# A graph layer with sorted segment sums: new round borders in the first part, a carried sum in one operation, and an earlier, thinner filling of the second table

## The chip, the cores and the metric

The kernel runs on one core of one Trainium2 chip. The metric is the device time of that core in microseconds; lower is better. The time before is 4865.99 us, the median of three runs (4857.05 to 4868.12).

Engine names are those of the profile: PE is TensorE (PEld its weight loads), DVE is VectorE, ACT is ScalarE, POOL is GpSimd and SP is SyncE, which here does nothing but start transfers. SBUF is the on-chip memory, PSUM the one that PE accumulates in.

## The reference

There are 12,500 nodes with 128 features and 412,500 edges with 64 features. The edge list is sorted by `dst`, not by `src`, and the sum runs over `src`.

```python
h, q, k, v = (node_features @ W + b for W, b in ((Wn, bn), (Wq, bq), (Wk, bk), (Wv, bv)))
eh = edge_features @ We + be
src, tgt = edge_index                      # stack([src, dst])
attn_in = concatenate([q[src], k[tgt], eh], axis=-1)
hmid = leaky_relu(attn_in @ A1 + b1, 0.2)
scores = leaky_relu(hmid @ A2 + b2, 0.2)
w = softmax(scores.mean(axis=-1), axis=0)  # over all edges
out = segment_sum(w[:, None] * v[tgt], src, num_segments=num_nodes)
y = h + out
y = gamma * (y - mean(y)) / sqrt(var(y) + 1e-5) + beta
result = layernorm(x + y)
```

## The kernel before

**Two stages that run at once.** Nodes are split into 98 blocks of 128 by their source number. Edges come in 403 groups of 1,024, which is eight tiles of 128 edges.

The *record stage* (`make`) goes through the 403 groups. For each edge it works out a record of 260 numbers: 128 of the edge's hidden sum without the query part, 128 of its value row, and the source's place within its block. PE multiplies one-hot matrices by table rows (`rows`, L931 and L936) into the PSUM tile `pkv`; ACT copies that into an SBUF tile `rec` of four edge tiles (`evacuate`, L946 and L947; six such buffers); POOL then writes each tile of 128 records to DRAM with one indirect transfer (L958), to the block of its source. The places come from running counts on PE and DVE (L851 to L913); `pcs`, in PSUM, is the running count for each block. A group thus costs POOL eight of these scatters.

The *sum stage* (`sums_of`) reads the records back, now sorted by block, and adds them up. Its work comes in *units*: up to three blocks, and of each block t tiles of 128 records. For a unit, SP loads the tile `rt` (L1150) and spreads the source numbers over the partitions (L1204). PE and DVE add the query rows (L1216, L1230, L1239), DVE and ACT apply the leaky ReLU (L1249, L1253), PE multiplies by A2 and sums the heads. Then comes a short chain: a maximum on DVE (`mx`, L1305), spread by PE (L1311), reduced on DVE (`m`, L1319, and `ref`, L1320), the exponential on ACT (`w`, L1329). ACT weighs one-hot matrices with `w` (L1352) and PE sums the value rows into `psm` (L1381). Pieces of at most four tiles go through these steps. A unit starts every eight steps of a hand-made plan (`lags`), whether it has 12 tiles or 15.

**Parts and rounds.** The 403 groups are cut into three *parts* (`PARTS`, L36), each with a table in DRAM (part three uses the first table again). A part is summed in *rounds*: when the records up to a stop are made, a round may sum those tiles of each block that are certain to be full by then. The stops are group numbers. The table below is what the code works out; "units" is blocks per unit times tiles per block.

| round | stop | units before | begins at group, before | stop after | units after | begins at group, after |
|---|---|---|---|---|---|---|
| 1 | 74 | 33 of 3x5 | 74 | 74 | 33 of 3x5 | 74 |
| 2 | 127 | 33 of 3x4 | 127 | 140 | 33 of 3x5 | 140 |
| 3 | 165 | 49 of 2x6 | 167.1 | 165 | 33 of 3x5 | 187.4 |
| 4 | 225 | 33 of 3x4 | 227.1 | 225 | 33 of 3x4 | 234.9 |
| 5 | 278 | 33 of 3x4 | 278 | 278 | 33 of 3x4 | 278 |
| 6 | 307 | 33 of 3x5 | 318.1 | 307 | 33 of 3x5 | 317.3 |
| 7 | 367 | 33 of 3x4 | 367 | 367 | 33 of 3x4 | 367 |
| 8 | 403 | 33 of 3x5 | after the last group | 403 | 33 of 3x5 | after the last group |

"Begins at" is `begun` (L1773 to L1777): the stop, or later if the round before is by an estimate not through. `PACE` (12 tiles a group) and the constant 2.7 are that estimate. The steps of a round are spread evenly over the groups between its beginning and the next one's, so a round's tiles divided by these groups is the density of sum work beside the record work. What is left at the last group runs alone, then round 8, then a closing stage with the two norms.

**The order.** Everything is issued in the order of the code (`manual_schedule`): the loop at L1796 goes through six points a group of the record stage, and puts the due fills, table steps and sum steps at each. Every engine works strictly in that order.

**Carried sums.** A round adds to what the rounds before it left in DRAM (`old`, L1362). The old sum must be scaled by the ratio of two reference maxima, `by`. `total` (L1384) does that with one DVE operation for each block (L1397): old times `by` plus the PSUM sum, 128x128 each. In round 1 there is no old sum and the PSUM tile is copied (L1391).

**Fills.** The top rows of each block in the two tables are zeroed beforehand, by 49 transfers each (`fill_piece`, L567 to L574) on SP's queue. The first table's come from SBUF; the second's come from a zeroed DRAM tensor, and were placed evenly from group 74 to group 163.

**Checks of the counts.** At a stop, DVE copies the running count `pcs` out of PSUM (`counted`, L993 to L996), and compares the copy with limits loaded four groups earlier (`gated`, `certain`, `ended`, L998 to L1014).

Of the kernel before, what the change touches and what calls it, by code (L numbers as in the profile page):

```python
# [10 lines left out]
FP = mybir.dt.float32  # L11
# [5 lines left out]
ALU = mybir.AluOpType  # L17
# [4 lines left out]
P = 128  # L22
# [10 lines left out]
ROWS = 3  # L33
XA = 3
SPAN = 42
PARTS = (74, 127, 165), (225, 278, 307), (367, 403)  # L36
NP = len(PARTS)
NR = sum(map(len, PARTS))
PACE = 12
TABS = 2  # L40
WIDTH = 15
BLK = 3
# [7 lines left out]
class Plan:  # L50
# [4 lines left out]
    def __init__(self, n, e, nb, groups):  # L55
        self.n, self.e, self.nb, self.groups = n, e, nb, groups
        at = lambda c: groups * c // 403
        ends = [at(part[-1]) for part in PARTS]
        self.parts = list(zip([0] + ends[:-1], ends))

        def means(g0, g1):
            return [
                (min(e, g1 * GT * P) - g0 * GT * P) * max(0, -(-(n - b) // nb)) / n
                for b in range(nb)
            ]
# [22 lines left out]
        for p, (g0, g1) in enumerate(self.parts):  # L88
            t0 = 0
            for g in map(at, PARTS[p][:-1]):  # L90
                t = int(min(m - 4.4 * m**0.5 for m in means(g0, g)) // P) - t0
# [380 lines left out]
def sorted_path(  # L472
# [8 lines left out]
    nc = tc.nc  # L481
# [3 lines left out]
    NBK = nb + 1  # L485
# [30 lines left out]
    for j, part in enumerate((1.0, -1.0)):  # L516
        nc.vector.tensor_scalar(
            A2s[:, H + 1 + j : H + 2 + j], A2s[:, H : H + 1], part * SLOPE / (1 - SLOPE), None,
            op0=ALU.mult,
# [6 lines left out]
    for j, part in enumerate((1.0, -1.0)):  # L526
        nc.vector.tensor_scalar(
            b2_r[:, H + 1 + j : H + 2 + j], b2_r[:, H : H + 1], part * SLOPE / (1 - SLOPE), None,
            op0=ALU.mult,
# [19 lines left out]
    zeros = dram.tile([P, fmax, WR], FP, name="zeros")  # L549
# [8 lines left out]
    def fill(k, n):  # L558

        b, top = 0, plan.tiles[k]  # L560
        while b < nb:
            m = 1
            while m < n and b + m < nb and plan.fill[k][b + m] == plan.fill[k][b]:
                m += 1
            a = plan.cap // P - plan.fill[k][b]
            if a < top:
                yield b, m, a, top - a  # L567
            b += m

    def fill_piece(k, b, m, a, f, source=None):  # L570
        cap = plan.cap
        piece = nc.sync.dma_start(
            out=rtab[k][b * cap : (b + m) * cap, :]
            .rearrange("(b c) w -> b c w", b=m)[:, a * P : (a + f) * P, :]  # L574
            .rearrange("b (p k) w -> p b (k w)", p=P),
            in_=(empty if source is None else source)[:, :f, :]
            .rearrange("p (o k) w -> p o (k w)", o=1)
            .to_broadcast([P, m, f * WR]),
        ).ins
        if k == 0 and source is None:  # L580
            tc.declare_no_dep(piece, group="rows0.0", reason="rows that no record has reached")
            tc.add_to_no_dep_group("fill0", piece)
# [29 lines left out]
    with tc.tile_pool(name="prep", bufs=1) as prep, tc.tile_pool(  # L612
        name="pprep", bufs=1, space=PSUM
# [107 lines left out]
    def spans():  # L721

        lim = const.tile([P, 2], FP)
        for i, (op, most) in enumerate(((ALU.max, SPAN - 1.0), (ALU.min, 0.0))):
            nc.vector.tensor_reduce(lim[:, i : i + 1], mm[:, i, :], AX.X, op)
            sign = 1.0 if op == ALU.max else -1.0
            nc.vector.tensor_scalar(
                bad[:, i : i + 1], lim[:, i : i + 1], sign, -sign * most, op0=ALU.mult, op1=ALU.add
            )
# [24 lines left out]
    def far(name, bufs, **k):  # L754
        return making.enter_context(tc.tile_pool(name=name, bufs=bufs, side="right", **k))

    one = far("one", 1)
# [30 lines left out]
    pcs = {}  # L788
    ready, made_rows = {}, [1]
    masks, placed, lims = {}, {}, {}  # L790
# [14 lines left out]
    def make(p):  # L805
# [183 lines left out]
        def worst(a, b, to, c):  # L989
            nc.vector.tensor_tensor(to, a, b, op=ALU.subtract)  # L990
            nc.vector.tensor_reduce(bad[:, c : c + 1], to, AX.X, ALU.max)

        def counted():  # L993
            runf = one.tile([P, NBK], FP, name="run")
            nc.vector.tensor_copy(runf, pcs[p])
            return runf  # L996

        def gated():  # L998

            runf = counted()  # L1000
            worst(runf, lims.pop(p)[0], runf, 3 + 2 * NR)

        def certain(r):

            runf = counted()
            worst(lims.pop(p)[0], runf, runf, 2 + 2 * r)

        def ended(r):

            runf = counted()  # L1010
            pcs.pop(p)
            low, over = lims.pop(p)
            worst(low, runf, low, 2 + 2 * r)
            worst(runf, over, over, 3 + 2 * r)  # L1014
            t = plan.rounds[r][3]
            masks[r] = maskp.tile([P, nb * max(placed)], BF, name="mask")
            nc.vector.tensor_tensor(
                masks[r][:, : nb * t].rearrange("p (b t) -> p b t", t=t),
                placed[t].rearrange("p (o t) -> p o t", o=1).to_broadcast([P, nb, t]),
                over[:, :nb].rearrange("p (b o) -> p b o", o=1).to_broadcast([P, nb, t]),  # L1020
                op=ALU.is_ge,
            )
# [40 lines left out]
    units = []  # L1063
# [48 lines left out]
    def sums_of(bp):  # L1112
# [273 lines left out]
        def total(i):  # L1386
            st, (p, bs, _) = state[i], units[i]
            m, psS = len(bs), st.pop("psS")
            if p == 0:
                st["old"] = oldp.tile([P, BLK, D], FP, name="old")  # L1390
                nc.vector.tensor_copy(  # L1391
                    st["old"][:, :m, :].rearrange("p u d -> p (u d)"), psS[:, P : (1 + m) * P]
                )
                return
            old, by = st["old"], st.pop("by")
            for u in range(m):
                nc.vector.scalar_tensor_tensor(  # L1397
                    old[:, u, :], old[:, u, :], by[:, u : u + 1],
                    psS[:, (1 + u) * P : (2 + u) * P], op0=ALU.mult, op1=ALU.add,
                )  # L1400
# [353 lines left out]
    def later():  # L1754

        for c in range(1, len(chunks)):
            yield from edges(tmp, c, CH // 2)
            yield
# [14 lines left out]
    begun, free_at = [], 0  # L1773
    for p, (_, g, _, t) in enumerate(plan.rounds):
        free_at = max(free_at, g)
        begun.append(free_at)
        free_at += sum(len(bs) * t + 2.7 for q, bs, _ in units if q == p) / PACE  # L1777

    with tc.manual_schedule():
        n1, n2, n3 = 6 * plan.rounds[0][1], 6 * plan.parts[1][0], 6 * G  # L1780
        n0 = n1 * 9 // 10
        fills = []
        for k, i0, i1, source in (0, 0, 6 * min(plan.gate, plan.rounds[0][1]) - 12, None), (
            1, n1, n2 - 12, zeros
        ):
            pieces = list(fill(k, 2))
            fills += [
                (i0 + (i1 - i0) * j // len(pieces), (k, *piece, source))
                for j, piece in enumerate(pieces)
            ]  # L1790
        fills = fills[::-1]
        tabs, made, nt = tables(), 0, 1 + (2 * ng - 1) * (NB + 7) + ng
        more, sent, ne = later(), 0, 11 * (len(chunks) - 1)
        done, r = 0, 0
        for i, _ in enumerate(_ for p in range(NP) for _ in make(p)):
            while fills and fills[-1][0] <= i:  # L1796
                fill_piece(*fills.pop()[1])
            while made < nt and made * n0 < i * nt:
                next(tabs, None)
                made += 1  # L1800
            while sent < ne and sent * n0 < i * ne:
                next(more, None)
                sent += 1
            if i == n1:
                for _ in tabs:
                    pass
                for _ in more:
                    pass
                spans()
                covered()  # L1810
                tab_pool.close()
                steps, starts = sums_of(pool("blk", BLKS))
            if i < n1:
                continue
            while r + 1 < NR and i >= 6 * begun[r + 1]:
                r += 1
            if r + 1 < NR:
                until = starts[r] + (starts[r + 1] - starts[r]) * (i - 6 * begun[r]) / (
                    6 * (begun[r + 1] - begun[r])
                )  # L1820
                while done < until:
                    for fn, args in steps[done]:
                        fn(*args)
                    done += 1
        while done < starts[-1]:
            for fn, args in steps[done]:
                fn(*args)
            done += 1
        making.close()
        for name, of, bufs, k in (  # L1830
            ("blk", "blk2", MORE, {}), ("end", "end", 4, {}), ("gamma", "gam", 1, {}),
            ("row", "row2", ROWS, {}), ("ph", "ph2", 2, dict(space=PSUM)),
            ("turn", "trn", 1, dict(space=PSUM)),
        ):
            late[name] = far(of, bufs, **k)
        for step in steps[done:]:
            for fn, args in step:
                fn(*args)
# [73 lines left out]
```

## Time and profile before

| what | value |
|---|---|
| median of three runs | 4865.99 us |
| the profiled execution, its time | 4862.14 us |
| the profiled execution, its span | 4860.4 us |
| first scatter begins, last scatter begins | 59.0 us, 4310.6 us |
| scatters (L958) | 3,224 |
| busy share of the span: PE, DVE, POOL, ACT | 83%, 84%, 68%, 64% |
| granted TensorE clock, mean | 0.927 |

How to read the rows in the next part. A row of the page's groups gives line, engine, operation, output and inputs, shape and count; after the bar the busy time in us and the mean ns of one; after the second bar the idle time of that engine just ahead of them and what ended it. A row of the windows gives a stretch of the span in us, then its length, then the busy time in us of each engine named in the header with the number of instructions in brackets, the granted clock, the share of the DMA engines that was busy, and GB/s. A row of the waits gives who waited for what, the total in us, how many times, and the longest.

All stages overlap, so a share of the whole span says little here. The windows by stage, and the waits of each stage, say more.

### The profile page before, as it was taken

The numbers are of one execution on the slowest core, as the hardware profiler recorded it, in microseconds if no ns is written. First come the engines' busy times: TensorE is split into PE (matmuls) and PEld (weight loads), VectorE is DVE, ScalarE is ACT, GpSimd is POOL, SyncE is SP. The second block draws the span as 40 slices with busy tenths as digits, with TensorE's granted clock in tenths as the row PEclk, the third lists the DMA queues.
The fourth block names the chain that finished last, engine by engine and source line by source line (L and its number), as shares of the span: only waits on it lengthen the run. The fifth ranks groups of instructions, "written<-read, shape, count | busy, mean of one in ns | idle before, by whom it ended". The sixth has DMA issues, their size and how long they took to land. (4 is left out here: it accounts for less than half of the span.)

```text
span 4860.4 us, 84339 instructions
## 1 busy us (share of the span) xinstructions
PE 4017.1 (83%) x26346; PEld 3094.3 (64%) x26626; DVE 4104.8 (84%) x8629; ACT 3110.9 (64%) x8211; POOL 3305.1 (68%) x3280
## 2 busy tenths in 40 slices
PE   3655665688888899999998888899899999998997
PEld 2434443566766666777676666666677777666776
DVE  8878886698888888889898888898999998977877
ACT  2332222477776667777776666676777777777886
POOL 4777777777777767777777777777777777731103
PEclk7777776799999999999999999999999999999999
DMA  6778876999999998999998888999999999989964
GB/s 197 265 252 266 269 266 214 335 358 346 350 338 346 363 337 307 310 321 313 322 313 311 301 295 301 322 338 321 329 337 329 340 322 322 339 286 329 324 222 162
DMA packets 608627, 1484.42 MB, mean 305 GB/s; under 512 B 101632, under 2 KB 309395, under 8 KB 606374
## 3 DMA queue, kind: packets, MB, share of 16 engines
q1 hardware_dynamic: 445822, 1049.05, 64.5%
q0 software_dynamic: 154752, 429.39, 23.2%
q8 instruction: 211, 3.46, 0.3%
q14 instruction: 250, 2.05, 0.1%
q10 hardware_dynamic: 7592, 0.48, 0.1%
HBM read 906.61 MB, written 611.06 MB: 312 GB/s over the span
## 5 line engine op out<-in xcount | busy, mean ns | idle before, releaser
L958 POOL DMA_INDIRECT rtab<-rec,idx x3224 | 3220.9, 999 | 1087.4 <-issue 775.9
L946 ACT ACTIVATE rec<-pkv 128x1024 f32<-128x1024 f32 x806 | 821.7, 1019 | 1090.4 <-DMA rtab<-rec,idx 557.5
L1352 ACT ACTIVATE ohw<-ohs,w 128x128 f32<-128x128 bf16 x3626 | 1187.0, 399 | 70.8 <-DVE ohs L1338 39.0
L1381 PE MATMUL psm<-rt,ohw 128*128 128x128 f32 x7252 | 1020.6, 284 | 3.0 <-ACT ohw L1352 2.5
L1381 PEld LDWEIGHTS psm<-rt,ohw 128*128 128x128 f32 x7252 | 934.6, 196 | 82.2 <-ACT ohw L1352 21.4
L936 PE MATMUL pkv<-WeS,eat 128*128 128x256 f32 x3224 | 932.3, 416 | 0.0
L1253 DVE TENSOR_TENSOR hm<-ph,hm 128x512 f32<-128x512 f32 (+1 forms) x932 | 625.0, 671 | 294.9 <-ACT hm L1249 292.8
L931 PE MATMUL pkv<-kvs,ohd 128*128 128x256 bf16 x3224 | 534.5, 293 | 325.9 <-ACT rec L946 319.6
L931 PEld LDWEIGHTS <-ohd 128*128 128x128 bf16 x3224 | 319.4, 105 | 581.0 <-issue 461.9
L936 PEld LDWEIGHTS pkv<-WeS,eat 128*128 128x128 f32 x3224 | 612.5, 211 | 72.2
L1230 PE MATMUL ph<-ident,rt 128*128 128x128 f32 x3626 | 581.3, 282 | 76.8 <-DVE hm L1253 74.8
L1230 PEld LDWEIGHTS ph<-ident,rt 128*128 128x128 f32 x3626 | 415.2, 145 | 304.5 <-issue 145.5
L1216 DVE TENSOR_SCALAR ohT<-rowB,iotaP,power 128x512 bf16<-128x512 uint8 (+3 forms) x1176 | 577.2, 509 | 30.1 <-DMA rowB<-row 30.0
L1249 ACT ACTIVATE hm<-ph 128x512 f32<-128x512 f32 (+1 forms) x932 | 532.6, 571 | 61.8 <-PE ph L1239 25.4
L872 DVE TENSOR_SCALAR ohd<-dstb,node 128x1152 bf16<-128x1152 uint8 x404 | 565.0, 1399 | 6.1 <-PE pkv L931 6.1
L1239 PE MATMUL ph<-ohT,qs 128*128 128x512 bf16 (+2 forms) x2072 | 495.3, 329 | 41.1 <-DVE ohT L1216 24.0
L900 DVE TENSOR_TENSOR ats<-pc,oh 128x792 f32<-128x792 f32 x403 | 392.0, 973 | 27.5 <-PE pc L880 27.5
L1264 PE MATMUL psc<-hm,A2s 128*32 128x512 f32 (+2 forms) x1864 | 370.1, 607 | 44.7 <-DVE hm L1253 33.7
L862 DVE TENSOR_REDUCE few<-oh 128x99 bf16<-128x792 bf16 x403 | 395.1, 980 | 13.9
L1338 DVE TENSOR_TENSOR ohs<-iotaE,sl 128x512 bf16<-128x512 bf16 (+1 forms) x932 | 395.2, 424 | 5.0 <-ACT ohw L1352 4.8
L911 DVE TENSOR_REDUCE pos<-ats 128x8 f32<-128x792 f32 x403 | 390.5, 969 | 1.9
L1329 ACT ACTIVATE w<-S,ref 128x12 f32<-128x12 f32 (+2 forms) x280 | 84.7, 302 | 340.6 <-DVE ref L1320 327.7
(193 smaller groups left out, 4072.3 us busy)
## 6 DMA issues: line engine op xcount, KB each, us to landing
rt<-rtab SPq DMA_DIRECT2D x177, 1560.0 KB
rt<-rtab SPq DMA_DIRECT2D x96, 1950.0 KB
eat<-in_ea SPq DMA_DIRECT2D x201, 512.0 KB
rtab<-rec,idx POOLq DMA_INDIRECT x3224
dstb<-dtab SPq DMA_DIRECT2D x201, 256.0 KB
qs<-qtab SPq DMA_DIRECT2D x224, 192.0 KB
atab<-old SPq DMA_DIRECT2D x224, 192.0 KB
rtab<-zeros SPq DMA_DIRECT2D x49, 780.0 KB
```

The costliest lines, as they stand in the source:

```text
L872: nc.vector.tensor_scalar(to, row[:, cols], node, None, op0=ALU.is_equal)
L931: nc.tensor.matmul(pk[:, i, h, :], ohd[t], kvs, start=(h == 0), stop=False,)
L936: nc.tensor.matmul(pk[:, i, :, :D], eat[:, (j + i) * P : (j + i + 1) * P], WeS, start=False, stop=True,)
L946: nc.scalar.activation(rec[:, :, :, : 2 * D], pk, AF.Copy)
L958: one_tile = nc.gpsimd.indirect_dma_start(out=rtab[p % TABS][:, :], out_offset=bass.IndirectOffsetOnAxis(ap=idxs[g][:, t : t + 1], axis=0) ...
L1216: nc.vector.tensor_scalar(st["oh"][k][:, (a - t0) * P : (b - t0) * P], st["rowB"][:, a * P : b * P], iotaP, power[:, bs[u] : bs[u] + 1], o ...
L1230: nc.tensor.matmul(ph[:, j * P : (j + 1) * P], st["rt"][:, t0 + j, :D], ident, is_transpose=True, start=(j == 0), stop=False,)
L1239: nc.tensor.matmul(ph[:, cols], st["qs"][:, j0 // t, s, :], oh[:, cols], start=False, stop=(s == 1 and j1 == t0 + n),)
L1249: nc.scalar.activation(hm, state[i]["ph", k][:, : n * P], AF.Copy, scale=SLOPE)
L1253: nc.vector.tensor_tensor(hm, ph[:, : n * P], hm, op=ALU.max)
L1352: nc.scalar.activation(ohw[:, j, :], ohs[:, :, j], AF.Copy, scale=st["w"][:, t0 + j : t0 + j + 1])
L1381: nc.tensor.matmul(st["psS"][:, (1 + u) * P : (2 + u) * P], ohw[:, j, :], st["rt"][:, t0 + j, D : 2 * D], start=(k == 0), stop=(k == t - 1),)
```

## The change

Four edits.

1. `PARTS`: the second stop moves from 127 to 140. All three rounds of part one then have five tiles a block, and units of the same three blocks. There are 264 units in place of 280; the tiles (3,626) are the same.
2. `total`: where a round and the one before it have the same number of blocks a unit (now all of them), one operation on 128x384 with the first block's `by` stands for three on 128x128. The three blocks of a unit share one reference, so their `by` is the same.
3. The fills of the second table are placed from group 10 to group 157, and sorted together with those of the first. Of the 49, 22 now stand ahead of the first load of the sum stage, where one stood before.
4. `counted` goes: the checks read `pcs` in PSUM directly and write over the limits. The estimate's constant is 2.4 in place of 2.7; with the stops this gives the right half of the table above.

```diff
-PARTS = (74, 127, 165), (225, 278, 307), (367, 403)
+PARTS = (74, 140, 165), (225, 278, 307), (367, 403)
...
-        def counted():
-            runf = one.tile([P, NBK], FP, name="run")
-            nc.vector.tensor_copy(runf, pcs[p])
-            return runf
-
         def gated():
 
-            runf = counted()
-            worst(runf, lims.pop(p)[0], runf, 3 + 2 * NR)
+            low = lims.pop(p)[0]
+            worst(pcs[p], low, low, 3 + 2 * NR)
...
         def ended(r):
 
-            runf = counted()
-            pcs.pop(p)
+            run = pcs.pop(p)
             low, over = lims.pop(p)
-            worst(low, runf, low, 2 + 2 * r)
-            worst(runf, over, over, 3 + 2 * r)
+            worst(low, run, low, 2 + 2 * r)
+            worst(run, over, over, 3 + 2 * r)
...
             old, by = st["old"], st.pop("by")
+            if min(BLK, WIDTH // plan.rounds[p][3]) == min(BLK, WIDTH // plan.rounds[p - 1][3]):
+                flat = old[:, :m, :].rearrange("p u d -> p (u d)")
+                nc.vector.scalar_tensor_tensor(
+                    flat, flat, by[:, 0:1], psS[:, P : (1 + m) * P], op0=ALU.mult, op1=ALU.add
+                )
+                return
             for u in range(m):
...
-        free_at += sum(len(bs) * t + 2.7 for q, bs, _ in units if q == p) / PACE
+        free_at += sum(len(bs) * t + 2.4 for q, bs, _ in units if q == p) / PACE
...
-            1, n1, n2 - 12, zeros
+            1, 60, n2 - 48, zeros
...
-        fills = fills[::-1]
+        fills = sorted(fills, key=lambda piece: piece[0])[::-1]
```

DVE, at one of the units of 3x4 in round 7, before. `S` and `mx` begin the chain of the maximum, `m` and `ref` end it; `oh`, `few`, `ohd`, `ats`, `pos`, `idx` belong to the record stage, and the rest to other units.

```order
L1300 SCALAR_TENSOR_TENSOR S<-sl,psm 128x12
L1305 TENSOR_REDUCE mx<-S 128x1
L1216 TENSOR_SCALAR ohT<-rowB,iotaP,power 128x512
L1253 TENSOR_TENSOR hm<-ph,hm 128x512
L1338 TENSOR_TENSOR ohs<-iotaE,sl 128x512
L900 TENSOR_TENSOR ats<-pc,oh 128x792
L1397 SCALAR_TENSOR_TENSOR old<-old,by,psm 128x128 x3
L1319 TENSOR_REDUCE m_52677<-psm 128x1
L1320 SCALAR_TENSOR_TENSOR ref<-m_52677,ref 128x1
```

The same unit now (lines have moved by five or six).

```order
L1294 SCALAR_TENSOR_TENSOR S<-sl,psm 128x12
L1299 TENSOR_REDUCE mx<-S 128x1
L911 TENSOR_REDUCE pos<-ats 128x8
L913 SCALAR_TENSOR_TENSOR idx<-pos,twin 128x8
L1210 TENSOR_SCALAR ohT<-rowB,iotaP,power 128x512
L1247 TENSOR_TENSOR hm<-ph,hm 128x512
L1332 TENSOR_TENSOR ohs<-iotaE,sl 128x512
L851 TENSOR_TENSOR oh<-blk,iotaE 128x792
L862 TENSOR_REDUCE few<-oh 128x99
L872 TENSOR_SCALAR ohd<-dstb,node 128x3x384
L1392 SCALAR_TENSOR_TENSOR old<-old,by,psm 128x384
L1313 TENSOR_REDUCE m_52180<-psm 128x1
```

The carried sum stands directly ahead of `m` in both; it is three operations before and one now, and which record operations fall between `mx` and `m` has shifted.

SP, in the first stage, some ten groups in, before. `rtab_76` is the first table, `rtab_77` the second; `kvs`, `dstb` and `eat` are loads of the record stage, four groups ahead of their use, and `kvtab` and `xt` belong to the making of the node tables.

```order
L1739 DMA kvtab<-sp 128x5376
L1711 DMA xt<-in_xN 128x896
L818 DMA eat<-in_ea 128x1024
L822 TENSOR_LOAD start
L827 ISA
L827 DMA kvs<-kvtab 128x256
L572 DMA rtab_76<-empty 128x2x780
```

The same place now.

```order
L1739 DMA kvtab<-sp 128x5376
L1711 DMA xt<-in_xN 128x896
L572 DMA rtab_77<-zeros 128x2x780
L818 DMA eat<-in_ea 128x1024
L822 TENSOR_LOAD start
L827 ISA
L827 DMA kvs<-kvtab 128x256
L572 DMA rtab_76<-empty 128x2x780
```

A fill of the second table now stands between the loads of the record stage, about one in three groups; nothing else has moved there.

More of the change, by code (lines that the diff above doesn't have):

```diff
@@ L991, in worst @@
             nc.vector.tensor_reduce(bad[:, c : c + 1], to, AX.X, ALU.max)
-        def counted():
-            runf = one.tile([P, NBK], FP, name="run")
-            nc.vector.tensor_copy(runf, pcs[p])
-            return runf
         def gated():
-            runf = counted()
-            worst(runf, lims.pop(p)[0], runf, 3 + 2 * NR)
+            low = lims.pop(p)[0]
+            worst(pcs[p], low, low, 3 + 2 * NR)
         def certain(r):
-            runf = counted()
-            worst(lims.pop(p)[0], runf, runf, 2 + 2 * r)
+            low = lims.pop(p)[0]
+            worst(low, pcs[p], low, 2 + 2 * r)
         def ended(r):
-            runf = counted()
-            pcs.pop(p)
+            run = pcs.pop(p)
             low, over = lims.pop(p)
-            worst(low, runf, low, 2 + 2 * r)
-            worst(runf, over, over, 3 + 2 * r)
+            worst(low, run, low, 2 + 2 * r)
+            worst(run, over, over, 3 + 2 * r)
             t = plan.rounds[r][3]
```

## The prediction

> **What bounds the kernel now.** I first read what paces the 4,250 us in which records are made, and ask POOL, whose scatters end it. The page's group, then the waits, then the scatter's own line:
>
> ```profile
> L958 POOL DMA_INDIRECT rtab<-rec,idx x3224 | 3220.9, 999 | 1087.4 <-issue 775.9
> ```
> ```profile
> POOL rtab L958 <- issue: 775.9, 2544, 0.8
> ```
> ```profile
> L958 POOL DMA_INDIRECT rtab<-rec,idx x3224: 954/960/2788, 59.0 to 4310.6; - x190
> ```
>
> A scatter takes 960 ns (median), and 2,544 times POOL then spends 775.9/2544 = 0.305 us on nothing that another engine could end. So a scatter cannot come more often than every 1.265 us, a group not faster than 8 x 1.265 = 10.12 us, and 403 groups not under 4,078 us. From first to last they take 4310.6 - 59.0 = 4251.6 us. POOL's own pace is the floor of nine tenths of the kernel; only 173 us there can be won at all, and the rest must come from the 550 us behind it.
>
> The windows by stage, for POOL's scatters alone (length, busy time and count), show where the 173 us lie. Length / count x 8 is the pace of a group.
>
> ```profile
> core 0: us, POOL busy (x), PEclk, DMA share, GB/s
> 59.00:440.00 381.00, 295.77 (x268) 0.77 0.79 258
> 440.00:825.00 385.00, 295.43 (x295) 0.73 0.78 260
> 825.00:1505.00 680.00, 519.01 (x527) 0.94 0.97 340
> 1505.00:1880.00 375.00, 267.94 (x272) 0.95 0.96 339
> 1880.00:2500.00 620.00, 465.39 (x469) 0.98 0.92 315
> 2500.00:2975.00 475.00, 362.81 (x369) 0.96 0.88 305
> 2975.00:3440.00 465.00, 352.61 (x360) 0.98 0.92 322
> 3440.00:3945.00 505.00, 386.96 (x388) 0.97 0.95 332
> 3945.00:4312.00 367.00, 274.93 (x280) 0.98 0.94 324
> ```
>
> The paces are 11.37, 10.44, 10.32, **11.03, 10.58**, 10.30, 10.33, 10.41 and 10.49 us. The two in bold, groups 136 to 229, are rounds two and three, which the change rebuilds. The slow first window has no sum work at all and another cause.
>
> Next, who waits there. First the stage at 10.30, from 2500 to 2975 us:
>
> ```profile
> ACT rec L946 <- DMA rtab<-rec,idx: 88.9, 40, 4.7
> ```
>
> ACT waits for a record buffer that POOL's scatter has not emptied: the engines are ahead, and POOL is the bound. Then 1505 to 1880:
>
> ```profile
> DVE sl L1177 <- DMA rt<-rtab: 20.5, 9, 5.6
> ...
> ACT rec L946 <- DMA rtab<-rec,idx: 16.9, 13, 4.5
> ...
> POOL rtab L958 <- ACT rec L947: 12.7, 13, 3.1
> POOL rtab L958 <- ACT slT L1194: 10.2, 6, 5.6
> ```
>
> Here POOL waits for ACT: the lead is used up, the other engines cannot make records fast enough beside the sums. Yet none is full. The windows of all engines for 12-tile units (2975 to 3440), for 15-tile units (3440 to 3945), and behind the records:
>
> ```profile
> core 0: us, PE busy (x) PEld busy (x) DVE busy (x) ACT busy (x) POOL busy (x), PEclk, DMA share, GB/s
> 1880.00:2500.00 620.00, 569.07 (x3913) 438.71 (x3961) 554.25 (x1166) 445.96 (x1235) 465.39 (x469) 0.98 0.92 315
> ...
> 2975.00:3440.00 465.00, 419.15 (x2786) 314.69 (x2820) 407.99 (x859) 324.92 (x902) 352.61 (x360) 0.98 0.92 322
> 3440.00:3945.00 505.00, 459.36 (x3317) 372.12 (x3352) 474.55 (x1018) 392.53 (x1041) 386.96 (x388) 0.97 0.95 332
> ...
> 4377.00:4717.00 340.00, 310.97 (x2439) 248.05 (x2470) 265.22 (x714) 288.90 (x847) 27.20 (x13) 0.99 0.84 290
> ```
>
> PE and DVE are 88 to 94% busy while records are made. What holds them back is the chain of a unit, by shape:
>
> ```profile
> L1329 ACT ACTIVATE w<-S,ref 128x12 f32<-128x12 f32 x177 | 53.3, 301 | 274.6 <-DVE ref L1320 268.9 <-DVE m L1319 5.3
> ...
> L1329 ACT ACTIVATE w<-S,ref 128x15 f32<-128x15 f32 x96 | 29.2, 304 | 57.8 <-DVE ref L1320 50.6 <-DVE m L1319 6.3
> ```
>
> A 12-tile unit leaves ACT idle for 274.6/177 = 1.55 us ahead of `w`, a 15-tile unit for 0.60 us. ACT also makes the records, so POOL starves behind it. That is the reason to expect something of this change: it turns 82 units of 12 tiles into 66 of 15.
>
> **Part by part.**
>
> *Rounds two and three.* They had 9.8 tiles a group (392 tiles in 40.1 groups, 588 in 60) and will have 490/47.4 = 10.33. Is that too dense? The nearest row is round six, 3440 to 3945: the same 15-tile units, 490/48.9 = 10.0 tiles a group, pace 10.41. There PE has 459.36/48.5 = 9.47 us and DVE 474.55/48.5 = 9.78 us of work a group. Were all of it sums, 10.33 tiles would add 3.3%, 0.3 us; records are in it too, and I take half: 9.63 and 9.94. Now the operations of 15-tile units:
>
> ```profile
> L1216 DVE TENSOR_SCALAR ohT<-rowB,iotaP,power 128x512 bf16<-128x512 uint8 x589 | 326.8, 555 | 30.1 <-DMA rowB<-row 30.0
> ...
> L1397 DVE SCALAR_TENSOR_TENSOR old<-old,by,psm 128x128 f32<-128x128 f32 x686 | 198.1, 342 | 47.1 <-PE psm L1381 45.5 <-ACT rec L946 1.1 <-issue 0.3
> L1216 DVE TENSOR_SCALAR ohT<-rowB,iotaP,power 128x256 bf16<-128x256 uint8 x293 | 113.6, 429 | 0.0
> ...
> L1216 DVE TENSOR_SCALAR ohT<-rowB,iotaP,power 128x384 bf16<-128x384 uint8 x195 | 96.5, 495 | 0.0
> ...
> L1216 DVE TENSOR_SCALAR ohT<-rowB,iotaP,power 128x128 bf16<-128x128 uint8 x99 | 49.5, 500 | 0.0
> ...
> L1391 DVE COPY old<-psm 128x384 f32<-128x384 f32 x32 | 17.6, 549 | 0.2 <-PE psm L1381 0.2
> ...
> L995 DVE COPY run<-pc 128x99 f32<-128x99 f32 x9 | 2.3, 253 | 11.0 <-PE pc L880 11.0
> ```
>
> Five tiles do not fall on pieces of four, so one-hots are cut: the two rounds had 196 of 512 and 98 of 256 columns (151 us) and get 66 of 512, 130 of 384, 130 of 256 and 66 of 128 (190 us): 39 us more of DVE. Sixteen units fewer save their few short operations, not counted here. This is no free lunch in busy time; the round-six row already contains the cut one-hots.
>
> *The carried sum.* 686 operations take 198.1 us (289 ns each, as they overlap). 231 wide ones, nearest to the copy of the same shape at 549 ns, take 127 us: 71 us of DVE saved over seven rounds, 0.31 us a unit. [...] The three stood directly ahead of `m`, in the chain that ACT waits for, so the gain is also latency there. At 0.69 units a group it takes rounds two and three to about 9.73 us of DVE, below round six as it ran. I therefore take that row's 10.41 us for both rounds: 375 - 272 x 10.41/8 = 21.1 us and 620 - 469 x 10.41/8 = 9.7 us, **30.8 us** together. Ends: 10.30 us (the best row) gives 41, the 10.58 of round three for both gives 15.
>
> *Rounds one and four.* Round one falls from 490/53 = 9.25 tiles a group to 7.4. It ran at 10.32 already, on POOL's floor: **0**. Round four rises from 7.7 to 9.1, still below the 9.8 of round five: from 10.30 to 10.33 on 369 scatters, **1.4 us lost**.
>
> *Rounds five to seven.* Five has 10.0 tiles a group for 9.8, with a shorter carried sum: 0. Six: 0. Seven ends without lead at 10.49; with units 0.3 us shorter and a lead from before I take 10.41: **2.6 us** (0 to 6.5).
>
> *Behind the records.* Round seven is estimated at 39.3 groups for 40.1, so at the last group 23 steps of it are left where 28 were (counted from the code). In 4312 to 4377 seven units went through (the window for `ref`, L1320, one a unit):
>
> ```profile
> 4312.00:4377.00 65.00, 1.12 (x7) 0.99 0.84 289
> ```
>
> That is 9.29 us a unit of eight steps, 1.16 us a step: five steps are **5.8 us**. Round eight is 91% PE and 85% ACT, and the carried sum on DVE is beside that: 0. Lead: if the engines are ahead of POOL at the last group, sums start that much sooner. Six buffers of four scatters are at most 6 x 4 x 1.265 = 30 us. Before there was about none, as the waits from 3945 to 4312 show:
>
> ```profile
> POOL rtab L958 <- ACT rec L947: 4.0, 7, 1.1
> ```
>
> I take **5 us** (0 to 25).
>
> *Fills.*
>
> ```profile
> rtab<-zeros SPq DMA_DIRECT2D x49, 780.0 KB
> ```
>
> 21 more of them stand in the first stage, where the DMA share is 0.79; the stage from 825 us ran at 0.97 with a fill every 1.8 groups and kept 10.32. So 0 there, and some relief for the late `rt` loads above (20.5 us), which is part of the 10.41. If the cover fails it is the second rival below.
>
> *Checks.* Nine copies of 0.25 us go; the next part's first count now waits for two subtractions in place of one copy. Limits are loaded 40 us ahead. 0.
>
> Sum: 30.8 - 1.4 + 2.6 + 5.8 + 5 = 42.8 us off the profiled execution's 4862.1 us, so 4819; that execution lies 3.9 us below the median of the runs, so **4823 us**.
>
> **The rivals.**
>
> *The gain is eaten by density.* If 10.33 tiles a group keep the engines as short of time as 9.8 did, rounds two and three run at (375 + 620)/(741/8) = 10.74 us as before, no lead survives, and 2.6 + 5.8 - 1.4 us are left: about 4859. For it: 1505 to 1880 starved at 9.8. Against it: 15-tile units ran at 10.41 with ACT waiting less.
>
> *Slower: the fills hold up the first stage.* Records, tables and 49 fills of the first table share SP's queue and the DMA engines there. If each of 21 fills (0.8 MB) keeps the scatters' data waiting for its own transfer, 2.35 us at 340 GB/s read or written once, 4.7 us if both count, that is 49 to 99 us; in the middle 4823 + 74 = 4897. It decides from 2.5 us a fill on. Against it: between the first two windows above the DMA share is equal (0.79, 0.78) while the pace goes from 11.37 to 10.44, so DMA load is not what slows the scatters there. [...]
>
> *Better still.* Everything from 1505 us on runs at 10.30, and the lead at the end is 20 us: 41 + 6.5 + 5.8 + 20 - 1.4 = 72, so 4794.
>
> **How the numbers follow.** Forecast 0.70 (its own range 4800 to 4850), better still 0.08, eaten 0.13, fills 0.09. A measurement of this kernel can tell about 0.2%, 9.7 us, from no change. Forecast and the better case are faster: 0.78. Eaten (4859) is the same: 0.13. Fills are slower: 0.09. The range goes from 4792, the better case, to 4868, which takes in the eaten gain; the fills are left out.
>
> **What would show it.** Right: scatters from group 136 to 229 at 10.4 us a group; POOL no longer waiting for ACT there, but ACT for record buffers; `w` with 128x15 on 162 units idle for about 0.6 us each; the carried sum 231 times at 0.5 to 0.6 us; the last scatter near 4277 us; the first two windows unchanged. Wrong: a pace above 10.6 in rounds two and three, or above 11.0 in the first 825 us, or a last scatter that is early with an end that is not.

## The result and the profile after

The changed kernel takes 4828.62 us, the median of four runs (4819.02 to 4832.61), against 4862.77 us (4857.05 to 4868.12, four runs): a ratio of 0.9924, 95% interval 0.9907 to 0.9941. It is faster by 34 us; 4823 us were forecast, with a range of 4792 to 4868. The profiled execution has a span of 4827.2 us, 33.2 us less than before.

POOL's scatters in the changed kernel, in windows that end with the stages; from the fourth on they hold the same groups as those of before, within two (length, busy time and count; length / count x 8 is the pace of a group):

```profile
core 0: us, POOL busy (x), PEclk, DMA share, GB/s
59.00:447.00 388.00, 300.51 (x273) 0.76 0.86 278
447.00:864.00 417.00, 318.72 (x319) 0.71 0.81 270
864.00:1505.00 641.00, 489.63 (x497) 0.88 0.90 305
1505.00:1856.00 351.00, 268.15 (x272) 0.96 0.96 333
1856.00:2467.00 611.00, 467.31 (x472) 0.97 0.96 337
2467.00:2951.00 484.00, 369.25 (x377) 0.97 0.94 327
2951.00:3425.00 474.00, 357.30 (x361) 0.99 0.95 331
3425.00:3922.00 497.00, 380.27 (x384) 0.98 0.95 330
3922.00:4284.00 362.00, 268.11 (x273) 0.98 0.93 324
4284.00:4827.00 543.00, 0.00 (x0) 0.96 0.75 261
```

Groups 136 to 229, where rounds two and three run, go from 11.03 and 10.58 us a group to 10.32 and 10.36, next to POOL's floor, estimated at 10.12. The first stage, groups 0 to 74, takes what it took (table below), at a DMA share of 0.86 and 0.81 where 0.79 and 0.78 stood. Two windows have lost: round five's, 2951 to 3425, goes from 10.33 to 10.50, and the last one from 10.49 to 10.61.

Who waits in 1505 to 1856 of the changed kernel; the row for `sl` is what was 20.5 us, the row for POOL what was 12.7 us:

```profile
ACT rec L946 <- DMA rtab<-rec,idx: 16.0, 9, 4.8
...
ACT w L1323 <- DVE ref L1314: 11.5, 10, 1.8
...
DVE sl L1171 <- DMA rt<-rtab: 5.9, 4, 2.9
...
POOL rtab L958 <- ACT rec L947: 1.2, 4, 0.3
```

POOL hardly waits for ACT there any more. ACT does not wait longer for record buffers, though, as was forecast with it (16.9 us before): the engines are ahead, but seldom by all six buffers. At the end POOL does wait for ACT, in 3922 to 4284, more than before (4.0 us in seven waits):

```profile
POOL rtab L958 <- ACT rec L947: 8.5, 13, 2.5
...
POOL rtab L958 <- ACT slT L1188: 6.4, 6, 4.8
```

The groups by shape: the wide carried sum, and `w` for units of 15 and of 12 tiles.

```profile
L1392 DVE SCALAR_TENSOR_TENSOR old<-old,by,psm 128x384 f32<-128x384 f32 x224 | 136.3, 609 | 36.3 <-PE psm L1375 35.5 <-PE pc L880 0.4 <-issue 0.2
...
L1323 ACT ACTIVATE w<-S,ref 128x15 f32<-128x15 f32 x160 | 48.4, 303 | 71.1 <-DVE ref L1314 65.2 <-DVE m L1313 3.4 <-ACT slT L1188 0.4
...
L1323 ACT ACTIVATE w<-S,ref 128x12 f32<-128x12 f32 x96 | 29.0, 302 | 159.8 <-DVE ref L1314 159.6 <-DVE m L1313 0.2
...
L1392 DVE SCALAR_TENSOR_TENSOR old<-old,by,psm 128x256 f32<-128x256 f32 x7 | 3.3, 474 | 1.0 <-PE psm L1375 1.0
```

ACT's idle time ahead of `w` is 71.1/160 = 0.44 us a unit of 15 tiles and 159.8/96 = 1.66 us a unit of 12. The second has not shrunk (1.55 before), though one operation now stands where three stood ahead of `m`.

Where the 33 us came from, from the start of each stage's first scatter in the two traces, and in a second execution of the changed kernel (the run `changed_again` below):

| groups, work beside them | before, us | after, us | second execution, us |
|---|---|---|---|
| 0 to 74, tables | 804.7 | 805.4 | 807.4 |
| 74 to 136, round one | 641.4 | 640.4 | 639.7 |
| 136 to 229, rounds two and three | 999.0 | 962.2 | 964.1 |
| 229 to 276, round four | 484.6 | 483.8 | 486.2 |
| 276 to 321, round five | 467.0 | 473.8 | 467.7 |
| 321 to 369, round six | 499.9 | 497.4 | 496.1 |
| 369 to the last scatter, round seven | 356.1 | 361.3 | 361.1 |
| behind the last scatter | 548.8 | 543.5 | 545.4 |

One stage gives 35 to 37 us, the end gives 3 to 5, and round seven takes 5 back. In one of the two executions round five loses 7 more.

The lead of the engines over POOL can be read from the traces too, as the time from the end of ACT's copy of a record buffer to that buffer's first scatter. A mean over ten groups, in us:

| from group | before | after | second execution | units of two blocks (below) |
|---|---|---|---|---|
| 110 | 18.9 | 19.7 | 19.9 | 20.2 |
| 160 | 0.9 | 11.9 | 13.3 | 1.0 |
| 190 | 1.4 | 10.8 | 16.5 | 0.9 |
| 250 | 19.7 | 4.8 | 18.7 | 1.5 |
| 310 | 1.1 | 1.1 | 9.2 | 0.8 |
| 390 | 0.9 | 0.9 | 1.4 | 1.1 |

Before, the lead was gone from group 140 to 230. Now it lasts through these rounds; at the end it is gone as before.

### The profile page after: what moved, and what is told of

Same layout as the page of the kernel before. It is cut to its first block, busy times and chain, and to the rows that moved or that the text cites. A ratio compares the mean times of both kernels' runs of the same rounds, so it can differ in the third digit from the quotient of the medians.

```text
span 4827.2 us, 84360 instructions
## 1 busy us (share of the span) xinstructions
PE 3991.6 (83%) x26680; PEld 3111.2 (64%) x26680; DVE 4064.7 (84%) x8217; ACT 3144.8 (65%) x8198; POOL 3304.4 (68%) x3279
## 5 line engine op out<-in xcount | busy, mean ns | idle before, releaser
L936 PE MATMUL pkv<-WeS,eat 128*128 128x256 f32 x3224 | 946.4, 421 | 0.0
L1210 DVE TENSOR_SCALAR ohT<-rowB,iotaP,power 128x512 bf16<-128x512 uint8 (+2 forms) x1274 | 598.9, 492 | 34.8 <-DMA rowB<-row 34.6
L1233 PE MATMUL ph<-ohT,qs 128*128 128x512 bf16 (+2 forms) x2548 | 559.7, 323 | 16.1 <-DVE ohT L1210 11.3
L1258 PE MATMUL psc<-hm,A2s 128*32 128x512 f32 (+1 forms) x1898 | 345.9, 607 | 31.9 <-DVE hm L1247 23.7
L1284 PEld LDWEIGHTS psm<-headsum,z 96*128 96x128 f32 (+2 forms) x2112 | 259.7, 193 | 32.8 <-issue 8.3
## 6 DMA issues: line engine op xcount, KB each, us to landing
dstb<-dtab SPq DMA_DIRECT2D x201, 256.0 KB
```

What stands on the lines that cost most here:

```text
L936: nc.tensor.matmul(pk[:, i, :, :D], eat[:, (j + i) * P : (j + i + 1) * P], WeS, start=False, stop=True,)
L1210: nc.vector.tensor_scalar(st["oh"][k][:, (a - t0) * P : (b - t0) * P], st["rowB"][:, a * P : b * P], iotaP, power[:, bs[u] : bs[u] + 1], o ...
L1233: nc.tensor.matmul(ph[:, cols], st["qs"][:, j0 // t, s, :], oh[:, cols], start=False, stop=(s == 1 and j1 == t0 + n),)
```

## The experiments

My theory, called the unit theory: what a unit costs beyond its tiles, above all the chain ahead of `w`, makes units of 15 tiles cheaper than units of 12, so the new stops carry the gain, by way of the lead. Its rivals: the VectorE theory (the saved VectorE work of the wide sum carries it) and the fill theory (the late loads of `rt` beside the fills were the trouble, and moving the fills carries it).

The runs went to three chips. On one, called the fast chip here (number 6), the kernel before takes 4860 us, as in the result above, whose chip is not on record. On the two others, called the slow chips (14 and 15), it takes 5881 and 5890 us, so only ratios can be compared between fast and slow. The kernel before has no trace on a slow chip.

**The stops alone** (slow chip 14, then slow chip 15).

```diff
-PARTS = (74, 127, 165), (225, 278, 307), (367, 403)
+PARTS = (74, 140, 165), (225, 278, 307), (367, 403)
```

> The kernel before with the stops 74, 140, 165 alone: 66 units of 15 tiles in rounds two and three, three operations for each carried sum, old fills, old constant. Unit theory (the gain is that 15-tile units leave ACT idle 0.4 to 0.6 us ahead of w where 12-tile units leave 1.55 us): faster by 15 to 25 us than before, groups 136 to 229 at 10.35 to 10.5 us, POOL not waiting for ACT there. VectorE theory (the gain is the 60 to 70 us of VectorE work that the wide sum saves): no gain or 0 to 10 us slower, since the cut one-hots add 39 us of VectorE work. Fill theory (late loads of rt beside the fills are what slows groups 136 to 170): 0 to 5 us faster, groups 140 to 163 still above 10.8 us.

Measured: 5861.16 us against 5881.43, ratio 0.9963 (0.9949 to 0.9977). The second time, with this expectation:

> The kernel before with the stops 74, 140, 165 alone, once more, on a chip where the scatters can be the bound. Unit theory: 15 to 25 us faster than before, scatters of groups 136 to 229 at 10.35 to 10.5 us, with a lead there of 5 us or more. VectorE theory: no gain, or slower. If the chip is one of the slow kind again: 18 to 25 us faster as in the first look.

Measured: 5869.86 us against 5890.47, ratio 0.9959 (0.9942 to 0.9976). Both are faster by 20 us, as the unit theory has it, though this adds VectorE work; as a theory of the whole gain the VectorE theory falls. But the way is another than the one foretold: on these chips the scatters are nowhere the bound, the lead is a mean of 1.4 us or less from group 80 on, and groups 136 to 229 run at 13.2 to 13.4 us.

**The wide sum alone, and the changed kernel without it** (slow chip 14; fast chip).

```diff
+            if min(BLK, WIDTH // plan.rounds[p][3]) == min(BLK, WIDTH // plan.rounds[p - 1][3]):
+                flat = old[:, :m, :].rearrange("p u d -> p (u d)")
...
```

> The kernel before with the wide carried sum alone; it applies in rounds two and five to eight, and rounds three and four keep the operation for each block, as the unit's blocks differ from the round before. Unit theory: 3 to 8 us faster, most of it at the end of the records, groups 136 to 170 still near 11 us. VectorE theory: 20 us faster or more, groups 136 to 170 under 10.7 us. Fill theory: 0 to 5 us faster.

Measured: 5879.22 us, ratio 0.9990 (0.9980 to 1.0001): at most 12 us, most likely 6.

> The changed kernel with three operations for each carried sum again. Unit theory: 3 to 10 us slower than the changed kernel, by less lead in rounds five and seven. VectorE theory: 20 us slower or more, groups 136 to 229 back above 10.55 us.

Measured: 4835.24 us (ratio to before 0.9949, 0.9930 to 0.9967) where the changed kernel takes 4828.79 beside it. The medians differ by 6.5 us, the intervals overlap. Groups 136 to 229 take 966.6 us against 964.1. The wide sum is worth some 6 us of the 34, if anything; the 58 us of VectorE work that it saves mostly lay beside other work.

**The fills alone, and all of them early** (slow chip 14; fast chip).

```diff
-            1, n1, n2 - 12, zeros
+            1, 60, n2 - 48, zeros
...
-        fills = fills[::-1]
+        fills = sorted(fills, key=lambda piece: piece[0])[::-1]
```

> The kernel before with the second table's fills from group 10 to 157 alone. Unit theory: 0 to 6 us faster; groups 136 to 170 between 10.8 and 11.0 us. VectorE theory: 0 to 3 us. Fill theory: 15 us faster or more, groups 136 to 170 at 10.5 us or below, and the wait of sl for rt there down from 20.5 us to under 8. The first 825 us no slower than before in the first two.

Measured: 5875.65 us, ratio 0.9997 (0.9984 to 1.0011). Nothing, on a chip where the scatters do not pace the kernel: POOL is idle ahead of them for 2,094 us in all here, and for 1,087 us in the kernel before where that takes 4860 us.

The other way round, the changed kernel with `1, 60, n1 - 12, zeros`:

> The changed kernel with all 49 fills of the second table between groups 10 and 72, beside those of the first. If a fill holds up the scatters of the first stage (the prediction's second rival): 27 more fills there cost 60 us or more, and the pace of the first 825 us goes above 11.2 us a group. If the scatters do not mind: within 5 us of the changed kernel, first 825 us unchanged, and the loads of rt in rounds one and two a little earlier.

Measured: 4828.96 us (ratio 0.9935, 0.9915 to 0.9954), the changed kernel's time. Its first stage, the windows of the scatters:

```profile
59.00:449.00 390.00, 299.46 (x273) 0.75 0.91 300
449.00:866.00 417.00, 318.81 (x320) 0.70 0.89 301
```

The DMA share goes to 0.91 and 0.89 and the pace stays at 11.43 and 10.43 us a group. The fills cost the scatters nothing measurable, with 22 or with all 49 of them in this stage. What the fill theory says of rounds two and three on the fast chip is not settled: with the old stops the fills were moved on slow chips only, and in the changed kernel the wait for `rt` fell from 20.5 to 5.9 us with stops and fills changed together.

**The estimate's constant back at 2.7** (slow chip 14).

```diff
-        free_at += sum(len(bs) * t + 2.4 for q, bs, _ in units if q == p) / PACE
+        free_at += sum(len(bs) * t + 2.7 for q, bs, _ in units if q == p) / PACE
```

> The changed kernel with the estimate's constant back at 2.7: rounds four to seven are spread a little thinner, and 28 steps in place of 23 are left at the last group. If the five steps cost what they were priced at: 4 to 6 us slower than the changed kernel, that is about 28 to 30 us faster than before. If work left over is only moved: within 2 us of the changed kernel, as the records' last groups run that much faster.

Measured: 5854.73 us, ratio 0.9942 (0.9923 to 0.9961). The changed kernel itself did not run on that chip, so this only says that all edits but the constant bring most of the gain. The five steps are read from the fast chip's traces: 548.8 us behind the last scatter before, 543.5 and 545.4 after. But round seven, which the constant packs denser, takes 356.1 us before and 361.3 and 361.1 after. Both stages together take 904.9 us before and 904.8 and 906.5 after, so on the fast chip the work looks moved, not saved.

**All but the stops** (slow chip 15).

```diff
-PARTS = (74, 140, 165), (225, 278, 307), (367, 403)
+PARTS = (74, 127, 165), (225, 278, 307), (367, 403)
```

> The changed kernel with the stops back at 74, 127, 165; the wide sum (in five rounds of seven), the early fills, the checks without copies and the constant 2.4 stay. Unit theory: 5 to 15 us faster than before, so that this and the stops alone add up to the whole, 30 to 35 us; groups 136 to 170 still above 10.7 us and no lead from there to group 230. Fill theory: 25 us faster or more, groups 136 to 170 under 10.5 us.

Measured: 5869.08 us, ratio 0.9963 (0.9948 to 0.9977). With the stops alone at 0.9959 the product is 0.9922, close to the whole change's 0.9924 in the result. So the halves add up, but the other edits bring as much as the stops, more than the 5 to 15 us expected. The wide sum (0.9990) and the fills (0.9997), each alone on chip 14, make 0.9987 together. What is left to 0.9963, some 0.0024, would be the constant and the checks, and the intervals are too wide to say which, or whether it is there at all.

The traces of chip 15 also put the gain of the stops in another place. Against this run, the stops alone take 794 us for 817 in groups 74 to 136, where round one has become thinner, 1242 for 1245 in groups 136 to 229, and 624 for 610 in groups 229 to 276, where round four has become denser. The two runs differ in the other edits too, but rounds two and three, which gained most on the fast chip, gained next to nothing here.

**The changed kernel again** (fast chip).

> The changed kernel once more, as the measure for the three beside it on this chip. On a chip like that of the first profiles: 0.990 to 0.995 of the kernel before, scatters of groups 136 to 229 at 10.3 to 10.4 us. On a chip like that of the last four runs, where the kernel before takes 5881 us and the scatters are seldom the bound: 0.992 to 0.996.

Measured: 4828.79 us, ratio 0.9927 (0.9907 to 0.9946).

**Units of two blocks in rounds two and three** (fast chip).

```diff
-        wide = max(1, min(BLK, WIDTH // t))
+        wide = 2 if p in (1, 2) else max(1, min(BLK, WIDTH // t))
```

> The changed kernel with units of two blocks (10 tiles) in rounds two and three: 98 units in place of 66, the same stops and nearly the same tiles a group. Unit theory: the idle time ahead of w and the fixed steps come back with the number of units, the lead that the first round builds is gone by group 160, POOL waits for ACT in rounds two and three, 25 to 60 us slower than the changed kernel. VectorE theory: 10 to 20 us slower (about 30 us of short VectorE operations and the carried sum in more pieces). Rival that only the thinner first round matters: within 5 us of the changed kernel.

In this run the carried sum in one operation, with the first block's `by`, also stands where the blocks of a unit come from two units of the round before, and so have two references.

Measured: 4993.46 us, ratio 1.0272 (1.0248 to 1.0296), 165 us slower than the changed kernel. The scatters of groups 136 to 170, 170 to 229 and 229 to 276:

```profile
1502.00:1880.00 378.00, 268.81 (x272) 0.97 0.88 297
1880.00:2572.00 692.00, 464.20 (x474) 0.97 0.85 288
2572.00:3092.00 520.00, 371.84 (x376) 0.97 0.91 314
```

11.1, 11.7 and 11.1 us a group. The waits from 1880 to 2572, and `w` by shape:

```profile
ACT w L1323 <- DVE ref L1314: 87.4, 49, 4.4
...
POOL rtab L958 <- ACT rec L947: 40.3, 27, 3.0
...
ACT rec L946 <- DMA rtab<-rec,idx: 26.3, 20, 3.3
```
```profile
L1323 ACT ACTIVATE w<-S,ref 128x10 f32<-128x10 f32 x101 | 30.5, 302 | 151.3 <-DVE ref L1314 151.3
```

The direction is the unit theory's, the size nearly three times its upper guess. The stops and the tiles are the same, and rounds two and three are even thinner (9.7 tiles a group in place of 10.3, as the estimate gives more units more room), yet groups 136 to 229 take 106 us more than in the changed kernel. The lead is spent there (table above), and groups 229 to 276 and 276 to 321, whose units are untouched, take 34 and 27 us more. Part of that is that round four begins at group 241.3 and not 234.9 and has 10.0 tiles a group for 9.1. That only the thinner first round matters is refuted.

The traces also show what a unit costs beside its tiles. Four TensorE operations come with each unit: the turning of its sources (L1187 before, L1181 now), the scores (L1264, L1258), the sum of the heads (L1290, L1284) and the spreading of the maximum (L1311, L1305). The two largest, in groups 136 to 229: before, in the second execution of the changed kernel, and with units of two blocks.

```profile
L1264 PE MATMUL psc<-hm,A2s 128*32 128x512 f32 x454 | 100.4, 615 | 12.8 <-DVE hm L1253 10.5 <-ACT slT L1194 2.3
L1290 PE MATMUL psm<-headsum,z 96*128 96x3 f32 (+1 forms) x600 | 74.4, 247 | 1.4 <-DVE old L1397 0.2
```
```profile
L1258 PE MATMUL psc<-hm,A2s 128*32 128x512 f32 (+2 forms) x508 | 79.7, 590 | 11.1 <-DVE hm L1247 6.8 <-ACT slT L1188 4.2
L1284 PE MATMUL psm<-headsum,z 128*128 128x4 f32 (+2 forms) x512 | 63.3, 247 | 13.5 <-DVE old L1392 7.0 <-ACT ohw L1346 5.3 <-DVE old L1385 1.1
```
```profile
L1258 PE MATMUL psc<-hm,A2s 128*32 128x512 f32 (+2 forms) x536 | 101.9, 549 | 9.9 <-DVE hm L1247 8.4 <-ACT slT L1188 1.0
L1284 PE MATMUL psm<-headsum,z 96*128 96x3 f32 (+2 forms) x696 | 92.5, 246 | 8.4 <-ACT z L1272 8.1
```

| groups 136 to 229 | before | changed, second execution | units of two blocks |
|---|---|---|---|
| time, us | 999 | 964 | 1070 |
| units (times their sources were turned) | 75 | 64 | 87 |
| the four operations, TensorE busy, us | 225.9 | 185.0 | 256.0 |
| TensorE busy in all, us | 906.5 | 877.1 | 952.5 |
| VectorE busy in all, us | 873.9 | 892.1 | 886.1 |

A unit thus takes 3.0, 2.9 and 2.9 us of TensorE, mostly with 12, 15 and 10 tiles in it. From before to now this falls by 41 us, and the stretch gets 35 us shorter; with units of two blocks it rises by 71 us, and the stretch gets 106 us longer. TensorE is 89 to 91% busy in all three. VectorE has the most work of the three in the fastest, which speaks against the VectorE theory once more. So most of what a unit costs is likely this TensorE work. No run changes these operations alone, and the profile models where a matmul ends, so this is argued and not shown.

**12-tile units with `w` one step later, and no steps left over** (slow chip 15).

```diff
+        ) if nk > 3 else dict(
...
+            reference=f + 2 + e, weights=f + 4 + e, old=f - 1, lowered=f + 7 + e,
+            select=f + 2 + e, weigh=f + 4 + e, add=f + 6 + e, total=f + 5 + e + L,
+            store=f + 8 + e + L,
```

> The changed kernel with w, weighing, summing, carried sum and store of each 12-tile unit one step later in the plan (rounds four, five and seven), which also puts the carried sum behind ref on VectorE. If the idle time of ACT ahead of w (1.66 us a 12-tile unit) is what makes 12-tile units eat the lead: the idle falls below 0.6 us a unit, the lead holds to group 310 and beyond 380, 5 to 15 us faster than the changed kernel. If 12-tile units are limited by something else: idle goes, time stays within 4 us.

Measured: 5881.94 us, ratio 0.9985 (0.9971 to 0.9999), so slower than the 0.9922 that the two halves give for the changed kernel on that chip. The idle time did go, to 1.7 us in all, where the stops alone had 142.8 on the same chip:

```profile
L1330 ACT ACTIVATE w<-S,ref 128x12 f32<-128x12 f32 x96 | 28.6, 298 | 1.7 <-issue 0.9 <-DVE ohs L1339 0.8
```
```profile
L1329 ACT ACTIVATE w<-S,ref 128x12 f32<-128x12 f32 x96 | 28.9, 301 | 142.8 <-DVE ref L1320 57.5 <-issue 44.8 <-DVE old L1397 31.7
```

Yet groups 229 to 276 take 644 us against 624 for the stops alone, though the constant 2.4 makes round four 4% thinner, and groups 276 to 321 take 618 against 603, with round five 2% denser. In the run of all but the stops, on the same chip and with the same density in round five, they take 608. So on this chip the idle time ahead of `w` is not what a 12-tile unit costs; the wait only moved.

The same with `begun[-1] = min(begun[-1], G)`:

> The same as late_w, and round seven spread so that none of its steps are left at the last group (23 before), 10.9 tiles a group. If steps are cheaper beside records than alone (1.16 us a step alone): the end behind the last scatter 20 to 27 us shorter, the last scatter 8 to 20 us later, 3 to 12 us faster than late_w. If they cost the same: within 3 us of late_w. If round eight's loads stall behind the last scatters: slower than late_w.

Measured: 5875.91 us, ratio 0.9976 (0.9962 to 0.9989). Behind the last scatter it takes 518.1 us for 543.5 of `late_w`, 25.4 less, and groups 369 to 402 take 480.0 for 449.6, 30.4 more. The median is 6 us lower, which the first of the three cases allows, but the intervals overlap and the two stages show no gain: on this chip, where the records leave no room, steps cost at least as much beside them as alone. No version here beats the changed kernel, as far as ratios from different chips can tell.

## Why the prediction was right, and where not

*The floor.* Right. No stage of the fast chip's traces goes below 10.12 us a group, 1.265 us a scatter, and the best run at about 10.3.

*Rounds two and three.* Right in size: 30.8 us foretold, 36.8 and 34.9 measured; the row of round six, 10.41, was a fair neighbour, and the pace came out at 10.32 to 10.38. That fewer units for the same tiles keep the lead is shown on the fast chip (`two_blocks`, the lead table). How much of the 36.8 us the stops bring alone is not: neither they nor the other edits ran alone there, and on the slow chips the other edits brought as much (0.9963 and 0.9959). What within a unit costs the time was argued from ACT's idle time ahead of `w`; `late_w` speaks against that for 12-tile units, on a slow chip, and on the fast chip it was not tried. What the prediction left out is TensorE's part of a unit. "Sixteen units fewer save their few short operations, not counted here" is said of VectorE there, and for TensorE it took 9.63 us of work a group, up from 9.47 in round six; 877.1 us over 93 groups are 9.43, as the operations of the units that are gone weigh 41 us. This would explain why the term was too small; no run tests it.

*The carried sum.* The term was mis-sized: 231 operations take 136.3 + 3.3 = 139.6 us, 609 ns each for three blocks and not 549, and save 58 us of VectorE (198.1 us before) and not 71. Each of the three on 128x128 took 342 ns on average before. The copy of the same shape, 549 ns, was a poor neighbour. That the saving was also latency in the chain shows faintly: ACT's idle time ahead of `w` is 1.43 and 1.66 us a 12-tile unit with the wide sum and 176.4/96 = 1.84 us without it, but it was 1.55 before.

*Round seven and the lead at its end.* These are the steps that failed. "With units 0.3 us shorter and a lead from before I take 10.41: 2.6 us" came out as 5 us lost, at 10.63 us a group; and the 5 us for a lead at the last group as none (0.9 and 1.4 us from group 390 on). Round seven is 2% denser than before, and its 12-tile units eat the lead as they did. Round five was put at 0 without asking what lead it starts with: that was 4.8 us in one execution and 18.7 in the other, and where it was small, round five lost 7 us.

*Behind the records.* 5.8 us for five steps: 5.3 and 3.4 measured. But the prediction booked the five steps as gone, and they went into round seven; the 5 us lost there are about what they cost, and the two stages together gained nothing.

*Fills and checks at nothing.* The first stage is unchanged within 3 us (804.7 us before, 805.4 and 807.4 after), and 27 fills more change it by nothing, at a DMA share of 0.91 and 0.89. That a fill does not hold up the scatters is measured for this stage; why it does not, no run shows. The relief for the `rt` loads, which was part of the 10.41, was not separated from the stops. By the ratios on the slow chips the checks and the constant together may be worth more than the 5.8 us given for the steps; not settled.

The sum of 42.8 us was nearly right in part by luck. The two failed terms, 7.6 us foretold and 5 us lost, were in part made good by rounds two and three, 4 to 6 us above their term. The range of 4792 to 4868 us took in the time before, 4866, so the table by stage says more than the range.

## What to carry to other kernels

Where one engine's issue rate is the floor of a long stage (here 1.265 us a scatter), ask in which stretches the others hold a lead over it: here round four took more work at no loss while a lead stood before it, and lost 34 us with units of two blocks, when none did. Count what a unit costs on every engine beside its tiles: here fewer, fuller units saved 41 us in TensorE's four operations of a unit in groups 136 to 229, and cutting VectorE's one-hots into more pieces for their sake was a good trade (VectorE's work there rose by 18 us in all). Work taken off the end of a stage has to be paid where it goes: here 3 to 5 us were won behind the records and 5 us lost in round seven. A lead that the next stretch needs should be read from the trace.

## What was not expected of the hardware

Two of the three chips took 1.21 times as long for the same program as the third (5881 and 5890 us against 4860). Single operations of VectorE, ScalarE and GpSimd have the same mean length there: in the stops alone on chip 15 and in the kernel before at 4860 us, a carried sum takes 342 and 342 ns, a copy to `rec` 1021 and 1019 ns, a scatter 996 and 999 ns. A matmul into `psm` for the values takes 296 ns on average where it takes 284 before. The waits of the stops alone on slow chip 15:

```profile
PEld L931 <- issue: 845.5, 454, 13.0
POOL rtab L958 <- ACT rec L947: 685.2, 221, 6.6
```

In the second execution of the changed kernel on the fast chip:

```profile
PEld L931 <- issue: 541.7, 335, 8.4
...
POOL rtab L958 <- ACT rec L947: 10.7, 30, 1.6
```

In these two runs, TensorE's granted clock is 0.86 on chip 15 and 0.92 on the fast chip. Engines also stand still there with no wait that the profile shows, counting pauses over 0.15 us: PE 524 times, 506 us in all, and ACT 300 times, 754 us (3 times, 2 us, and 27 times, 58 us, on the fast chip). So it is not TensorE alone. POOL then waits for records nearly everywhere, and the lead never forms; yet the whole change is worth the same 0.8% as far as its two halves tell. That fits a gain that comes from less work better than one that comes from the lead alone. Why the engines pause there was not found.
